# Moving one block of the softmax sums from TensorE to GpSimd, and the FFN bias adds from GpSimd to VectorE

## The chip, the cores and the metric

The kernel runs on one core of a Trainium2 chip. Its time is the device time of one launch in microseconds (us). TensorE is called PE here, VectorE DVE, ScalarE ACT, GpSimd POOL, and SyncE, which issues most DMAs, SP. A difference is told as a share of the time before.

## The reference

A "macaron" layer over 16 sequences of 512 tokens and width 128: half an FFN, causal attention with 16 heads and a latent of 32, half an FFN. Each part has its own layer norm and a residual.

```python
def ffn(x):   # weights rounded to int4, plus a low-rank term
    return einsum('bsd,df->bsf', x, int4(kernel)) + bias + einsum('bsr,rf->bsf', einsum('bsd,dr->bsr', x, a), b)

def attn(x):
    q = einsum('bld,dhk->blhk', x, Wq); lat = einsum('bld,dc->blc', x, Wkv_down)
    k, v = einsum('blc,chk->blhk', lat, Wk_up), einsum('blc,chk->blhk', lat, Wv_up)
    p = softmax(where(causal, einsum('bqhd,bkhd->bhqk', q, k) / 8, -inf))
    return einsum('bqhd,hdo->bqo', einsum('bhqk,bkhd->bqhd', p, v), Wout)

x = x + 0.5 * ffn(layernorm(x))
x = x + attn(layernorm(x))
x = x + 0.5 * ffn(layernorm(x))
```

## The kernel before

**Work and steps.** All is float32. A sequence has four blocks of 128 queries (or keys), and its 16 heads form four groups of four heads. Two groups make a pair, so there are 32 pairs. A pair takes five steps (`STEP`), and the loop over `n` walks through the 160 steps of all pairs. Step `n` computes scores with the queries on the partitions for pair `at(n)`; DVE finds their row maxima (`find_maxima`, L642 and L646, tile `nmax`). Six steps later (`LAG`) the scores are computed again with the keys on the partitions, the maxima are folded in, and ACT takes the exponentials (`exponentials`, L655, tiles `pt`). POOL sets the upper triangle of diagonal blocks to zero (`zeros`, L668, an affine select). PE's part of a step is one `burst` (L632); behind it stand other products: values (tile `o`), sums (tile `s`), projections (`yp`), queries (`qt_ps`), FFN products (`fp_a`, `fp_c`).

**The sums.** A softmax needs the sum of the probabilities over the keys. POOL first adds the tiles of different key blocks, and PE then sums over the partitions with a matrix of ones (`sum_products`, L754, tile `s`). The causal mask leaves query block i with i+1 key blocks. For one group, PE streams: block 0 of `pt0` (128 columns for each of four heads), the three blocks of `b01` (384 columns), which holds key blocks 0 and 1 and, in its middle block, also key block 2; and `b23` (128 columns), which holds key blocks 2 and 3 for the last queries. The products of `b01` and `b23` add up in the same PSUM columns for these queries. POOL makes `b01` with `add_01` (L738, two adds of 128x768) and `add_2` (L743), and `b23` with `add_23` (L748). A pair has `u` = 0 (its first group) and `u` = 1.

**After the sums.** ACT copies them (`ssb`), SP moves them through DRAM in several DMAs, DVE takes reciprocals (L822), SP spreads them over the partitions (`rb`), and POOL multiplies (`normalise`, L830, tile `ot`).

**The FFNs.** `front(b)` (first FFN, letter a) and `tail(b)` (second FFN, letter c) are generators whose pieces are hung into the steps by `plan` and by lists such as `FRONT_STEPS` and `TAIL_STEPS`. `with_bias` (L379, tile `xb`, 128x512) adds the bias to the residual. In `front` it stands in a step of its own, 28 steps ahead of the sequence's first. In `tail` it stands in the same step as `turn_blocks` (L366), the transpose that makes `xt_c`, and ahead of it; the product `fp_c` (L385) reads `xt_c` and stands behind the next burst, and DVE then makes `x3` from `fp_c` and `xb` (L397). Each engine works through its instructions in the order in which the program issues them. `ln_newton` (L344 to L346, tiles `e_w`, `r_w`) is a chain of three small DVE instructions, once per sequence.

**Buffers that matter here.** The score tiles `sx` have two buffers of two PSUM banks; all other PSUM tiles share four banks in turn (`ps_t`). `b01`, `b23` and `xb` have two buffers each.

Of the kernel before, what the change touches and what calls it, by code (L numbers as in the profile page):

```python
# [14 lines left out]
ALU = mybir.AluOpType  # L15
# [10 lines left out]
def macaron_kernel(  # L26
# [14 lines left out]
    nc = tc.nc  # L41
# [43 lines left out]
    def load_x(b):  # L85
        x_sb = io.tile([P, NT, D], F32, tag="x", name=f"x_{b}")
        nc.sync.dma_start(x_sb, x[b].rearrange("(t p) d -> p t d", p=P))
        return x_sb
# [234 lines left out]
    def ln_stats(src, ln, what, blocks):  # L323
        c = COLUMNS[what]
        for t in blocks:
            nc.vector.bn_stats(ln["stats"][:, c + t, :], src[:, t, :])
        for t in blocks:
            nc.vector.bn_aggr(ln["mv"][:, c + t, :], ln["stats"][:, c + t, :])
# [48 lines left out]
    def with_bias(src, name, engine):  # L377
        xb = act2.tile([P, NT, D], F32, tag="xb", name=f"xb_{name}")
        engine.tensor_tensor(xb, src, bias_bc, ALU.add)  # L379
        return xb  # L380
# [25 lines left out]
    def ln_of(what, b):  # L406
        w = b + {"c": 2, "b": -2, "a": -3}[what]
        if w not in lns:
            lns[w] = ln_tile(f"w{w}")
        return lns[w]  # L410
# [10 lines left out]
    def front(b, st):  # L421


        x_sb, z = xs.pop(b), zs.pop(b)
        na, nb = f"a{b}", f"b{b}"
        la = ln_of("a", b) if b > 2 else early["a", b]
        lb = ln_of("b", b) if b > 1 else early["b", b]
        ln_stats(x_sb, la, "a", (0, 1))
        yield
        ln_stats(x_sb, la, "a", (2, 3))  # L430
        if b > 1:
            yield
        if 0 < b < B - 1:
            xs[b + 1] = load_x(b + 1)
            zs[b + 1] = load_blocks(x[b + 1], f"a{b + 1}")
        yield
        if b == 0:
            xt = turn(x_sb, na, "xt_a")
            yield
        xb = with_bias(x_sb, na, nc.gpsimd if b > 1 else nc.vector)  # L440
        yield
        if b:
            xt = turn_blocks(z, na, "xt_a")
            yield
        x1 = st["x1"] = ffn(xt, la, xb, na, "x1", 5)
        yield
        ln_stats(x1, lb, "b", (0, 1))
        yield
        ln_stats(x1, lb, "b", (2, 3))
        yield  # L450
        xn = ln_scale(x1, nb, lb)
        if b:
            there = to_dram(xn, nb)
            yield
            z = load_blocks(there, nb)
        yield
        xnt = turn_blocks(z, nb, "xnt_b") if b else turn(xn, nb, "xnt_b")
        yield
        mp = take(f"kt_ps_{b}")
        kt = st["kt"] = act2.tile([P, L], F32, tag="kt", name=f"kt_{b}", bufs=3)  # L460
        if b == 0:
            product(mp, wkv4_flat, xnt)
            nc.vector.tensor_copy(kt, mp)
        else:

            for j in range(NT):
                nc.tensor.matmul(
                    mp[ts(j, LD), :P], lhsT=wkv4_flat[:, :LD], rhs=xnt[:, ts(j, P)], start=True, stop=True,
                    skip_group_check=True,
                )  # L470
            kt4 = act2.tile([P, P], F32, tag="kt4", name=f"kt4_{b}", bufs=1)
            nc.vector.tensor_copy(kt4, mp[:, :P])
            yield
            kt_d = dram.tile([P, P], F32, tag="kt_d", name=f"kt_d_{b}", bufs=2)
            nc.sync.dma_start(kt_d, kt4)
            yield
            for h in range(HG):
                nc.sync.dma_start(
                    kt[ts(h, LD), :].rearrange("c (j n) -> c j n", j=NT), kt_d.rearrange("(j c) n -> c j n", j=NT)
                )  # L480

        def query(g):
            mp = take(f"qt_ps_{b}_{g}")
            product(mp, wqk_flat[:, ts(g, P)], xnt)
            if g % 2 == 0:
                st["qt", g] = act2.tile([P, 2, L], F32, tag="qt", name=f"qt_{b}_{g}", bufs=4)
            nc.scalar.copy(st["qt", g - g % 2][:, g % 2, :], mp)  # L487

        yield
        query(0)  # L490
        yield
        query(1)
        yield
        query(2)
        yield
        query(3)
        yield
# [18 lines left out]
    def tail(b, st, late=False):  # L516


        x2 = io.tile([P, NT, D], F32, tag="x2", name=f"x2_{b}")
        nm = f"c{b}"  # L520
        ln = ln_tile(nm) if late else ln_of("c", b)
        for half in (0, 1):
            yp = take(f"yp_{b}_{half}")[:, : 2 * D]
            for t in (0, 1):
                for g in range(NG):
                    product(yp[:, ts(t, D)], st["ot"][:, g, ts(2 * half + t, P)], wvo[:, g, :],
                            t == 0 and g == 0, g == NG - 1)
            nc.vector.tensor_tensor(
                x2[:, ts(half, 2), :], yp.rearrange("p (t d) -> p t d", d=D), st["x1"][:, ts(half, 2), :], ALU.add
            )  # L530
            if half and not late:
                there = to_dram(x2, nm)
            yield
            ln_stats(x2, ln, "c", (2 * half, 2 * half + 1))
            yield
        if late:
            xt = turn(x2, nm, "xt_c")
            yield
            ln_rstd(ln, "c")
            yield  # L540
            ln_newton(ln, "c")
        else:
            z = load_blocks(there, nm)
            yield
        xb = with_bias(x2, nm, nc.gpsimd)
        yield
        if not late:
            xt = turn_blocks(z, nm, "xt_c")
            yield
        x3 = ffn(xt, ln, xb, nm, "x3", 3)  # L550
        if not late:
            yield
        nc.sync.dma_start(out[b].rearrange("(t p) d -> p t d", p=P), x3)
        yield
# [190 lines left out]
    def add_23(st, g, u):  # L745

        both = st["b23", g + u] = probs.tile([P, HG, P], F32, tag="b23", name=f"b23_{st['b']}_{g + u}")
        nc.gpsimd.tensor_tensor(both, st["pt", 2, g][:, 2 + u], st["pt", 1, g + u][:, 0], ALU.add)  # L748

    def blocks(dst, w, tile_, start=False):  # L750

        for h in range(HG):
            mv = tile_[:, :, h, :]
            nc.tensor.matmul(  # L754
                dst[ts(h, LD), :].rearrange("p (b n) -> p b n", n=P), lhsT=w[h] if isinstance(w, list) else w,
                rhs=mv, start=start, stop=True, skip_group_check=True,
            )
# [14 lines left out]
            st["osb", g + u] = act2.tile([P, L], F32, tag="osb", name=f"osb_{st['b']}_{g + u}", bufs=4)  # L772
            nc.scalar.copy(st["osb", g + u], o_ps)  # L773

    def sum_products(st, g, u, s_ps):
        g1, w = g + u, ones_f[:, :LD]
        blocks(s_ps[:, :P], w, st["pt", 0, g1][:, :1], start=True)
        blocks(s_ps[:, P:], w, st["b01", g1])
        blocks(s_ps[:, 384:], w, st["b23", g1].unsqueeze(1))

    def sums(st, g, u):

        b, g1 = st["b"], g + u
        s_ps = take(f"s_{b}_{g1}")
        sum_products(st, g, u, s_ps)
        ssb = act2.tile([P, L], F32, tag="ssb", name=f"ssb_{b}_{g1}", bufs=3)
        nc.scalar.copy(ssb, s_ps)
        sums_d = dram.tile([HG, L], F32, tag="sums", name=f"sums_{b}_{g1}")
        for h in range(HG):
            nc.sync.dma_start(sums_d[h : h + 1], ssb[h * LD : h * LD + 1, :])  # L790
        st["sums", g1] = small.tile([P, HG * L // P], F32, tag="sum", name=f"sum_{b}_{g1}")
        nc.sync.dma_start(st["sums", g1], sums_d.rearrange("h n -> (h n)").rearrange("(p n) -> p n", p=P))
# [73 lines left out]
    N = len(groups)  # L866
    STEPS = len(STEP)
# [83 lines left out]
    def due(n, k, lag=LAG):  # L951

        at_ = at(n, lag + k)
        return at_ if at_ and (n - lag - k) % STEPS == 0 else None
# [5 lines left out]
    def ready_work(n):  # L960

        if n < N * STEPS and due(n, 10):
            st, g = due(n, 10)
            normalise(st, g + 1)
        for u in range(2):
            if due(n, 2 + 3 * u):
                st, g = due(n, 2 + 3 * u)
                add_01(st, g + u, 0)
                add_01(st, g + u, 1)
            if due(n, 3 + 2 * u):  # L970
                add_2(*due(n, 3 + 2 * u), u)
            if due(n, 3 + u):
                add_23(*due(n, 3 + u), u)

    for n in range(N * STEPS):
        parts(n - 0.5)
# [16 lines left out]
        for u in range(2):  # L993
            if due(n, 6 + 2 * u):
                st, g = due(n, 6 + 2 * u)
# [6 lines left out]
    n = N * STEPS  # L1002
# [24 lines left out]
    next(late_tail)  # L1027
    o_ps, s_ps = bank("o_late"), bank("s_late")
    values(st, g, 0, o_ps)
    sum_products(st, g, 0, s_ps)  # L1030
    normalise(st, gp)
    divided(turned(st)[:, g, :], o_ps, s_ps)

# [70 lines left out]
```

## Time and profile before

| what | value |
|---|---|
| time, median of 3 runs | 813.44 us (812.99 to 813.50) |
| the profiled execution: its time, its span | 811.2 us, 809.5 us |
| mean granted TensorE clock | 0.984 |
| ACT busy | 488.1 us (60%) |
| PE, products of `s` from `b01` and `b23` (L754) | 65.1 us busy, 992 records |
| POOL `add_01`, 128x768 (L738) | 126 instructions, mean 1820 ns |
| POOL `normalise` (L830) | 62 instructions, mean 1275 ns, 30.4 us idle before them for the DMA of `rb` |

The times and rows of the profile come from the profiled execution. A group's row gives the busy time, then the mean duration of one instruction, then the idle time of the engine before these instructions and what ended it. A float32 matmul leaves two records. A matmul's records overlap with the next ones', so starts tell more than durations there. In a timeline the first column is the start and the second the duration of a run of equal instructions.

### The profile page before, as it was taken

Reading aid. Unit: us, or ns where it says so; the run is one execution under the profiler, and the core shown is the slowest. Engines: PE = TensorE matmul, PEld = TensorE weight load, DVE = VectorE, ACT = ScalarE, POOL = GpSimd, SP = SyncE. Lnnn points to the kernel's source line nnn. Section 1 sums busy time; section 2 is a strip of 40 time slices with the busy share of each in tenths; the row PEclk is TensorE's granted clock in tenths of the full one; section 3 lists DMA queues with packets and bytes.
Section 4 is the critical chain, followed back from the end, with each engine's and each line's share of the span. In section 5 each row is a group of like instructions: output and inputs, shape, how many; then the busy total and the mean of one; then the engine's idle time right before and its main releaser. Section 6 shows DMA issues by size and latency. Waiting matters only on the chain.

```text
span 809.5 us, 35716 instructions
## 1 busy us (share of the span) xinstructions
PE 785.4 (97%) x15400; PEld 508.6 (63%) x15400; DVE 618.8 (76%) x1317; ACT 488.1 (60%) x971; POOL 677.6 (84%) x676
## 2 busy tenths in 40 slices
PE   7899999999999999999999999999999999999986
PEld 5646566676666667666666666566666766666544
DVE  7787886878778697777879787777878777686716
ACT  1247675757566675756667575666657566575652
POOL 1018989999998999989999998989989989989991
PEclk7899999999999999999999999999999999999998
DMA  6123122233322324232332323223122222211211
GB/s 138 28 60 65 35 69 68 62 72 77 91 64 67 85 58 93 64 82 60 82 84 56 88 60 83 73 70 83 51 67 68 50 72 70 60 45 56 45 38 34
DMA packets 171022, 54.01 MB, mean 67 GB/s; under 512 B 119512, under 2 KB 162680, under 8 KB 170864
## 3 DMA queue, kind: packets, MB, share of 16 engines
q1 hardware_dynamic: 170096, 51.44, 26.9%
q8 instruction: 120, 1.97, 1.0%
q10 hardware_dynamic: 768, 0.30, 0.2%
q14 instruction: 38, 0.31, 0.1%
HBM read 37.90 MB, written 13.80 MB: 64 GB/s over the span
## 4 chain that ended last, share of the span: by engine, by line
PE 77%; DVE 7%; DMA 4%; ACT 4%; POOL 4%; issue 2%; SPq 1%; DVEq 0%; POOLq 0%; ACTq 0%
PE sx L632 18%; PE o L754 15%; PE tx L632 14%; PE s L754 8%; PE yp L385 6%; PE qt_ps L385 6%; DVE nmax L642 2%; POOL b L738 2%; PE fp_a L385 2%; PE fp_c L385 2%; ACT xn_b L355 2%; DMA rb<-recs 2%; DMA recs<-rec 2%; ACT pt L655 1%; POOL ot L830 1%
## 5 line engine op out<-in xcount | busy, mean ns | idle before, releaser
L642 DVE TENSOR_REDUCE nmax<-sx 128x2 f32<-128x768 f32 (+2 forms) x384 | 312.6, 863 | 104.9 <-PE tx L632 66.8
L655 ACT ACTIVATE pt<-tx 128x512 f32<-128x512 f32 x616 | 319.5, 598 | 86.0 <-PE tx L632 78.8
L632 PE MATMUL sx<-kt,qt 32*128 32x512 f32 (+3 forms) x2048 | 323.4, 442 | 0.0
L632 PE MATMUL tx<-qt,kt 32*128 32x512 f32 x1728 | 319.2, 469 | 0.0
L738 POOL TENSOR_TENSOR b<-pt,pt 128x768 f32<-128x768 f32 x126 | 226.7, 1820 | 0.5
L632 PEld LDWEIGHTS sx<-kt,qt 32*128 32x128 f32 x2048 | 176.0, 185 | 24.4 <-issue 0.4
L668 POOL TENSOR_SCALAR_AFFINE_SELECT pt<-pt 128x1024 f32<-128x1024 f32 (+1 forms) x162 | 144.8, 899 | 19.8 <-ACT pt L655 17.6
L754 PE MATMUL o<-pt,lat 128*32 128x512 f32 x1984 | 146.4, 435 | 0.8 <-POOL pt L668 0.8
L632 PEld LDWEIGHTS tx<-qt,kt 32*128 32x128 f32 x1728 | 131.5, 185 | 5.1
L754 PEld LDWEIGHTS o<-pt,lat 128*32 128x32 f32 x1984 | 62.5, 109 | 77.9 <-issue 59.0
L632 PE MATMUL tx<-rows,ones_u 6*128 6x512 bf16 (+1 forms) x988 | 109.7, 297 | 1.0 <-DVE wvo L292 0.5
L830 POOL TENSOR_TENSOR ot<-osb,rb 128x512 f32<-128x512 f32 x62 | 79.1, 1275 | 30.5 <-DMA rb<-recs 30.4
L646 DVE TENSOR_REDUCE nmax<-sx 128x4 f32<-128x1024 f32 x64 | 75.4, 1219 | 31.7 <-PE tx L632 31.4
L773 ACT COPY osb<-o 128x512 f32<-128x512 f32 x62 | 36.3, 585 | 92.1 <-PE o L754 92.1
L632 PE MATMUL sx<-eye_b,mask_w 32*128 32x64 bf16 (+1 forms) x2560 | 87.6, 183 | 2.7 <-DVE nmax L646 1.7
L632 PEld LDWEIGHTS <-ones_u 6*128 6x128 bf16 x1024 | 43.1, 92 | 74.3 <-issue 61.6
L632 PEld LDWEIGHTS <-mask_w 32*128 32x128 bf16 x2560 | 67.3, 92 | 32.9 <-issue 24.7
L743 POOL TENSOR_TENSOR b<-b,pt 128x512 f32<-128x512 f32 x63 | 80.5, 1278 | 5.1
L748 POOL TENSOR_TENSOR b<-pt,pt 128x512 f32<-128x512 f32 x63 | 80.4, 1277 | 0.1
L385 PE MATMUL qt_ps<-xnt_b_b,wqk 128*32 128x512 f32 x512 | 68.0, 603 | 0.2
L754 PE MATMUL s<-b,ones_f 128*32 128x384 f32 x992 | 65.1, 380 | 2.2 <-POOL b L743 2.1
L487 ACT COPY qt<-qt_ps 128x512 f32<-128x512 f32 x64 | 37.5, 586 | 47.3 <-PE qt_ps L385 47.2
(193 smaller groups left out, 818.0 us busy)
## 6 DMA issues: line engine op xcount, KB each, us to landing
rb<-recs SPq DMA_DIRECT2D x248, 64.0 KB
x<-in_x_dram SPq DMA_DIRECT2D x16, 256.0 KB
sums<-ssb SPq DMA_DIRECT2D x248, 2.0 KB
z_a<-in_x_dram SPq DMA_DIRECT2D x60, 64.0 KB
blocks_b<-xn_b SPq DMA_DIRECT2D x15, 256.0 KB
z_b<-blocks_b SPq DMA_DIRECT2D x60, 64.0 KB
kt<-kt_d SPq DMA_DIRECT2D x60, 64.0 KB
out_dram<-x_c SPq DMA_DIRECT2D x15, 256.0 KB
```

Of the source, the lines that this page charges most:

```text
L385: nc.tensor.matmul(dst[ts(h, LD), :], lhsT=w[:, ts(h, LD)], rhs=mv, start=start, stop=stop, skip_group_check=True)
L487: nc.scalar.copy(st["qt", g - g % 2][:, g % 2, :], mp)
L632: nc.tensor.matmul(dst, lhsT=w, rhs=mv, start=first, stop=last, skip_group_check=True)
L642: nc.vector.tensor_reduce(nmax[:, i, heads, u], sx[:, :, col : col + (i + 1) * P], AX.X, ALU.max, negate=True)
L646: nc.vector.tensor_reduce(nmax[:, 1, heads, :], sx.rearrange("p k (u n) -> p k u n", u=2), AX.X, ALU.max, negate=True)
L655: nc.scalar.activation(pt[:, :, 2 * pair + k, :], tx[k].rearrange("p (b n) -> p b n", n=P), AF.Exp)
L668: nc.gpsimd.affine_select(diag, diag, pattern=[[0, diag.shape[1]], [1, P]], compare_op=ALU.is_ge, fill=0.0, base=0, channel_multiplier=-1,)
L738: nc.gpsimd.tensor_tensor(*flat, ALU.add)
L743: nc.gpsimd.tensor_tensor(b01, b01, st["pt", 2, g][:, u], ALU.add)
L748: nc.gpsimd.tensor_tensor(both, st["pt", 2, g][:, 2 + u], st["pt", 1, g + u][:, 0], ALU.add)
L754: nc.tensor.matmul(dst[ts(h, LD), :].rearrange("p (b n) -> p b n", n=P), lhsT=w[h] if isinstance(w, list) else w, rhs=mv, start=start, sto ...
L830: nc.gpsimd.tensor_tensor(turned(st)[:, g, :], st["osb", g], st["rb", g], ALU.mult)
```

## The change

For the first group of a pair (`u` = 0), and only inside the loop over `n`, POOL adds `b23` onto the last block of `b01` in place (`add_0123`), issued behind the `add_23` of that step; the sums of that group then leave out the product of `b23`. Sums of second groups, and of the very last pair (`late`), are as before. The bias adds of both FFNs move from POOL to DVE: all of `front`, and those of `tail` but the one of sequence 14 (`late`). The first two of `front` were on DVE already.

```diff
-        xb = with_bias(x_sb, na, nc.gpsimd if b > 1 else nc.vector)
+        xb = with_bias(x_sb, na, nc.vector)
...
-        xb = with_bias(x2, nm, nc.gpsimd)
+        xb = with_bias(x2, nm, nc.gpsimd if late else nc.vector)
...
+    def add_0123(st, g):
+
+        b01 = st["b01", g][:, 2]
+        nc.gpsimd.tensor_tensor(b01, b01, st["b23", g], ALU.add)
...
-    def sum_products(st, g, u, s_ps):
+    def sum_products(st, g, u, s_ps, late=False):
         g1, w = g + u, ones_f[:, :LD]
         blocks(s_ps[:, :P], w, st["pt", 0, g1][:, :1], start=True)
         blocks(s_ps[:, P:], w, st["b01", g1])
-        blocks(s_ps[:, 384:], w, st["b23", g1].unsqueeze(1))
-
-    def sums(st, g, u):
+        if u == 1 or late:
+            blocks(s_ps[:, 384:], w, st["b23", g1].unsqueeze(1))
+
+    def sums(st, g, u, late=False):
...
                 add_23(*due(n, 3 + u), u)
+        if due(n, 3) and n < N * STEPS:
+            add_0123(*due(n, 3))
...
-    sum_products(st, g, 0, s_ps)
+    sum_products(st, g, 0, s_ps, True)
```

More of the change, by code (lines that the diff above doesn't have):

```diff
@@ L778, in sum_products @@
         blocks(s_ps[:, P:], w, st["b01", g1])
-        blocks(s_ps[:, 384:], w, st["b23", g1].unsqueeze(1))
-    def sums(st, g, u):
+        if u == 1 or late:
+            blocks(s_ps[:, 384:], w, st["b23", g1].unsqueeze(1))
+    def sums(st, g, u, late=False):
         b, g1 = st["b"], g + u
         s_ps = take(f"s_{b}_{g1}")
-        sum_products(st, g, u, s_ps)
+        sum_products(st, g, u, s_ps, late)
         ssb = act2.tile([P, L], F32, tag="ssb", name=f"ssb_{b}_{g1}", bufs=3)
```

## The prediction, made before the changed kernel ran

> **What bounds the kernel now.** I read the page's busy times first, then PE's groups by form, the timeline around one sums stage, PE's own waits, and last the timelines of DVE and POOL at the places where the bias adds are to stand.
>
> ```profile
> PE 785.4 (97%) x15400; PEld 508.6 (63%) x15400; DVE 618.8 (76%) x1317; ACT 488.1 (60%) x971; POOL 677.6 (84%) x676
> ```
>
> PE is busy for 97% of the span. That alone could be overlap of records, so I looked at starts: over all 62 stages of `o`, for instance, the time from the stage's start to the next stage's start is 2.18 to 2.64 us with a median of 2.29, that is, PE issues without holes. Its listed waits are small:
>
> ```profile
> PE s L754 <- POOL b L743: 2.1, 5, 1.0
> PE sx L632 <- DVE nmax L646: 1.7, 1, 1.7
> ```
>
> (total us, times, longest.) So a stage taken from PE shortens the program unless something new comes late. POOL's `b` is the only input that PE waited for several times, so POOL is the engine to watch.
>
> **What the change removes from PE.** A sums stage of a first group:
>
> ```profile
> 420.89 0.43 PE L754 MATMUL s<-pt,ones_f 128*32 128x128 f32 x8
> 421.14 1.05 PE L754 MATMUL s<-b,ones_f 128*32 128x384 f32 x16
> 422.00 0.41 PE L385 MATMUL mt<-ident_b,terms 128*32 128x128 bf16 x16
> ```
>
> From start to start the products of `b01` and `b23` take 422.00 - 421.14 = 0.86 us for 384 + 128 columns, so the 128 that go take a quarter, 0.215 us; the 128 of `pt` take 0.25 by the same reading. Other ends: 24.9 us busy for the 62 products of this form is 0.40 each, but that includes the drain under which the next stage already runs. I take 0.215. There are 31 such stages (32 pairs less the last): 31 x 0.215 = 6.7 us (7.8 by 0.25).
>
> **What POOL gains and loses.** Rows: `add_0123` has the form of L743.
>
> ```profile
> L743 POOL TENSOR_TENSOR b<-b,pt 128x512 f32<-128x512 f32 x63 | 80.5, 1278 | 5.1
> L379 POOL TENSOR_TENSOR xb_a<-x,bias_sb 128x512 f32<-128x512 f32 x14 | 17.8, 1268 | 17.8 <-DVE x_a L397 17.8
> L379 DVE TENSOR_TENSOR xb_a<-x,bias_sb 128x512 f32<-128x512 f32 x2 | 1.4, 684 | 0.0
> ```
>
> Added 31 x 1.278 = 39.6 us, removed 28 bias adds (14 of each FFN) x 1.268 = 35.5; net 4.1 of 677.6. In the order of instructions a bias add goes from in front of `add_01` of the first group, and the new add comes behind `add_23` of the same group, so within most pairs POOL runs 1.27 us ahead in between and is back in place after it. Where no bias add goes (the first pairs, some of the last), POOL is 1.3 us late from the new add on. Who waits for that: the sums of `u` = 0, one burst later. Between the end of `add_23` and PE's start on `b01` there are 1.81 us in the tightest of the 31 pairs (68.59 to 70.41) and up to 5.7, so 1.3 fits. Behind the new add queue the small casts of `terms`, the next select, `ot` and the second group's adds. There the cover is a wait that POOL has anyway:
>
> ```profile
> 447.46 1.28 POOL L830 TENSOR_TENSOR ot<-osb,rb 128x512 f32<-128x512 f32 x1 [1.50 <-DMA rb<-recs]
> ```
>
> This wait is 0.3 to 2.3 us in most pairs; PE then has 0.05 to 1.8 us until it needs the second group's `b01`. Without cover a pair would lose up to 1.3.
>
> **What DVE gains.** 28 x 0.684 = 19.2 us at 76% busy. But does an add of two SBUF tensors run at that pace beside POOL? The two above ran while POOL was idle. The trace has such instructions beside POOL's adds, the `e_w` chain:
>
> ```profile
> 424.48 3.62 POOL L738 TENSOR_TENSOR b<-pt,pt 128x768 f32<-128x768 f32 x2
> 426.27 1.85 DVE L344 SCALAR_TENSOR_TENSOR e_w<-mv_w,y_w 128x12 f32<-128x12 f32 x1
> 428.17 1.29 POOL L743 TENSOR_TENSOR b<-b,pt 128x512 f32<-128x512 f32 x1
> 428.37 1.13 DVE L346 SCALAR_TENSOR_TENSOR r_w<-e_w,y_w 128x12 f32<-128x12 f32 x1
> ...
> 796.25 0.16 DVE L344 SCALAR_TENSOR_TENSOR e_c<-mv_c,y_c 128x4 f32<-128x4 f32 x1 [4.10 <-ACT y_c L339]
> ```
>
> L344 takes 0.16 us with POOL idle and 1.85 here: it ends at 428.12, as POOL's second add ends at 428.10. L346 ends with L743. So a DVE instruction with two SBUF inputs that finds a POOL add running waits for its end, up to 1.82 us, and gets in ahead of the next. Whether POOL's add in turn waits for a long DVE instruction, these 0.16 us ones cannot show: between nothing and 0.68 us per bias add. I take the whole; POOL is then 0.69 us late per pair instead of level, which the wait for `rb` covers in all but about the last two pairs.
>
> [...]
>
> **The first FFN's add** is issued behind the transpose of `xnt_b`, at about 408.3 in the pair at 400. POOL's add of 128x768 will then run from 407.7 to 409.5, so the bias add ends near 410.1, and the four maxima of the step, 409.65 to 412.13 before, end at 413.3. PE's next burst starts at 413.26 on the buffer whose maxima come first (by 412.3). Cover 1 us; without it the burst waits. No cost.
>
> **The second FFN's add** is the tight one, for the transpose of `xt_c` is right behind it, and `fp_c` waits for that.
>
> ```profile
> 429.42 2.34 DVE L646 TENSOR_REDUCE nmax<-sx 128x4 f32<-128x1024 f32 x2
> 430.88 1.09 POOL L668 TENSOR_SCALAR_AFFINE_SELECT pt<-pt 128x1024 f32<-128x1024 f32 x1 [0.83 <-ACT pt L655]
> 431.68 0.70 DVE L366 STREAM_TRANSPOSE xt_c_c<-z_c 128x512 f32<-128x512 f32 x1
> 431.94 1.27 POOL L379 TENSOR_TENSOR xb_c<-x,bias_sb 128x512 f32<-128x512 f32 x1
> 434.13 1.08 PE L385 MATMUL fp_c<-w_mid,xt_c_c 128*32 128x128 f32 x32
> ```
>
> DVE comes to it at 431.68, while POOL's select runs until 431.97; POOL's next add of 128x768 now starts right there. In the 14 places DVE is there 0.2 to 0.9 us before the select's end. Whether the select holds it or not, it is ahead of the add: bias add until 432.65 at the latest, transpose until 433.3, 0.8 us before `fp_c`. The maxima start at 433.45 instead of 433.09, which nothing feels. Three of the 14 have only 0.2 us, and bursts now come 0.2 earlier; for those and for the uncovered last pairs I charge 0.6.
>
> **Sum.** 811.2 - 6.7 + 0.6 = 805.1 for an execution like the profiled one. That one is 2.2 us below the median of the runs; against 813.44 the forecast is 807.3.
>
> **Rivals.**
> 1. *The second FFN's add comes behind POOL's add (slower).* If DVE arrives after the select's end, it waits 1.82, ends at 434.4, the transpose at 435.0: `fp_c` is 0.9 late. Behind it the maxima and `x3` end at 438.7 instead of 436.6, and the burst's second half, due at 437.07 + 0.9, takes over `fp_c`'s bank: 0.7 more. 1.6 x 14 = 22 us, so 829 if it hits every sequence, 818 if half. It decides at a shift of 0.2 to 0.9 us between DVE and POOL. For it: the `e_w` chain just ahead, itself held by POOL, sets DVE's arrival. Against: the shift is on the good side in all 14. 0.25.
> 2. *The second groups' sums come late:* the cover by the wait for `rb` fails since that DMA chain does not get faster with PE. PE's gain of 0.215 per pair then goes into the wait of L754 for L743, plus up to 0.7 in pairs without slack: 813 to 818. Against: the wait is POOL's, not PE's, in 29 of 62. 0.08.
> 3. *The gain is real and elsewhere eaten to nothing,* DVE at 79% holding `sx` a little longer in each sequence: 0.24 each in 28 places is 6.7, so 813.4. 0.05.
>
> **Chances.** Forecast 0.62. A measurement here tells about 0.2%, 1.6 us, from no change. Faster: 0.62 and a little of rival 1 where few places are hit, 0.64. Within 0.2%: rival 3 and some of 2, 0.07. Slower: 0.29. Range: from 805.0 (7.8 us gained, nothing lost, rounded down) to 820, which takes in rivals 2 and 3 and half of rival 1; about 0.15 is left out above.
>
> **What would show it.** Right: 248 records fewer of the 128x128 product `s<-b`; first groups' stages 0.64 us from `b01` to the next stage; POOL's L379 nearly gone; DVE's `xb_a` near 1.8 us, `xb_c` near 1; the step from `fp_c`'s stage before to `fp_c` unchanged. Wrong: `xb_c` above 2 us and PE waiting for DVE before `fp_c` (rival 1), or PE's wait of L754 for L743 well above 2.1 us (rival 2).

## The result, and the profile after

The changed kernel has a median of 811.41 us in 20 runs (809.42 to 813.75), the kernel before 813.38 in 20 (810.78 to 814.91): ratio 0.9981, interval 0.9972 to 0.9990. It is faster by about 1.6 to 2.0 us. The sum forecast 6.1. The direction came out, two thirds of the gain did not.

The page's row of engines (busy us, share, instructions):

```profile
PE 782.2 (96%) x15152; PEld 503.0 (62%) x15152; DVE 646.9 (80%) x1345; ACT 486.3 (60%) x971; POOL 691.1 (85%) x679
```

PE has 248 records fewer, as forecast, DVE 28 us more. A first group's stage in the timeline of PE:

```profile
422.42 0.43 PE L759 MATMUL s<-pt,ones_f 128*32 128x128 f32 x8
422.66 0.83 PE L759 MATMUL s<-b,ones_f 128*32 128x384 f32 x8
423.31 0.41 PE L385 MATMUL mt<-ident_b,terms 128*32 128x128 bf16 x16
```

From `b01` to the next stage it is 423.31 - 422.66 = 0.65 us, 0.86 before. Compared stage by stage with the trace of before, PE comes 0.215 us earlier at every one of these places but the first, that of pair 0, where the next stage waits. So the gain was there and was given back elsewhere. PE's waits (total us, times, longest):

```profile
PE s L759 <- POOL b L743: 4.4, 8, 1.0
...
PE mt L385 <- POOL terms L723: 1.7, 3, 1.0
...
PE o L759 <- POOL pt L668: 1.5, 3, 1.0
```

Before, these were 2.1, 1.2 and 0.8. The first is the wait that the prediction put up as the sign of its rival 2. The list takes in only part of it, since PE's weight loads wait too (for the same `b` 4.3 us before and 7.3 after). Taken instead as the step from the product of `pt` to that of `b01` in the second groups' sums, less 0.24 (undisturbed it is 0.22 to 0.24), the delay sums to 3.5 us before and 6.2 after. Below this is the second groups' delay. In both traces 1.2 us of it are those of the last such sums, at 777 us. POOL's own waits:

```profile
POOL terms L719 <- DVE nmax L642: 47.6, 1, 47.6
POOL ot L836 <- DMA rb<-recs: 21.2, 22, 1.7
```

The wait for `rb` is still there (30.4 before). In the pairs where POOL waits for it, POOL is not late by its own work. All delayed pairs but the last, ten of them, are of this kind: POOL stood idle for 0.9 to 1.7 us before the `ot` that precedes their adds.

The spans of the two profiled executions, 811.1 us and 809.5, would say that the changed kernel is slower. They differ at the head. These are windows of the trace; after the span come the busy times of PE, PEld, DVE, ACT and POOL, then the granted clock, DMA share and GB/s; first before, then after:

```profile
26.00:34.00 8.00, 7.07 (x105) 3.54 (x104) 4.95 (x12) 2.18 (x5) 0.00 (x0) 1.00 0.21 35
```

```profile
26.00:34.00 8.00, 7.33 (x84) 3.01 (x83) 3.37 (x10) 1.67 (x4) 0.00 (x0) 0.79 0.21 35
```

The granted clock was 1.00 in one and 0.79 in the other, and PE is 2.6 us later at 42 us. Of the experiments below, e11 (bias adds on POOL) had 0.79 there too, e10 (bias adds on DVE) 1.00. So it is no effect of the change, and PE's progress is compared from behind the head on.

### The profile page after: what moved, and what is told of

Read it like the earlier page. It is cut to its first block, busy times and chain, and to the rows that moved or that the text cites. A ratio compares the mean times of both kernels' runs of the same rounds, so it can differ in the third digit from the quotient of the medians.

```text
span 811.1 us, 35275 instructions
## 1 busy us (share of the span) xinstructions
PE 782.2 (96%) x15152; PEld 503.0 (62%) x15152; DVE 646.9 (80%) x1345; ACT 486.3 (60%) x971; POOL 691.1 (85%) x679
## 4 chain that ended last, share of the span: by engine, by line
PE 61%; POOL 16%; DVE 9%; DMA 5%; ACT 3%; issue 3%; SPq 2%; POOLq 0%; DVEq 0%; ACTq 0%
PE sx L632 14%; PE o L759 12%; PE tx L632 11%; POOL b L738 7%; PE yp L385 6%; PE s L759 5%; PE qt_ps L385 5%; DVE nmax L642 3%; DMA rb<-recs 3%; POOL pt L668 2%; POOL b L743 2%; POOL ot L836 2%; PE fp_a L385 2%; SPq L833 1%; ACT xn_b L355 1%
## 5 line engine op out<-in xcount | busy, mean ns | idle before, releaser
L642 DVE TENSOR_REDUCE nmax<-sx 128x2 f32<-128x768 f32 (+2 forms) x384 | 310.3, 858 | 78.9 <-PE tx L632 45.9
L738 POOL TENSOR_TENSOR b<-pt,pt 128x768 f32<-128x768 f32 x126 | 235.0, 1885 | 2.7
L759 PE MATMUL s<-b,ones_f 128*32 128x384 f32 x744 | 58.4, 416 | 4.5 <-POOL b L743 4.4
```

Source lines behind the costliest of these rows:

```text
L642: nc.vector.tensor_reduce(nmax[:, i, heads, u], sx[:, :, col : col + (i + 1) * P], AX.X, ALU.max, negate=True)
L738: nc.gpsimd.tensor_tensor(*flat, ALU.add)
L759: nc.tensor.matmul(dst[ts(h, LD), :].rearrange("p (b n) -> p b n", n=P), lhsT=w[h] if isinstance(w, list) else w, rhs=mv, start=start, sto ...
```

## The experiments

Ratios are to runs of the kernel before taken beside those of the experiment, with 95% intervals. "Drift" is by how much a stage of PE starts later than in the trace of before.

**Which part gives the gain back?** e1 is the new add alone:

```diff
-        xb = with_bias(x_sb, na, nc.vector)
+        xb = with_bias(x_sb, na, nc.gpsimd if b > 1 else nc.vector)
...
-        xb = with_bias(x2, nm, nc.gpsimd if late else nc.vector)
+        xb = with_bias(x2, nm, nc.gpsimd)
```

> The new add and the shorter first-group sums alone; both bias adds stay on POOL as in the kernel before. POOL gets 31 x 1.28 = 40 us more and nothing back. Theory (POOL's chain makes the second groups' sums late): the whole 1.28 us now stands in front of the second group's adds, so PE's waits for them grow by more than in the changed kernel (there from 3.5 to 6.2 us): 812 to 818, ratio 0.998 to 1.006. Rival A (the loss is at DVE's places: the head's xb_a in front of xt_a, about 1 us, and the bursts): these are as before here, so the gain is larger than the changed kernel's: 807 to 809, ratio 0.992 to 0.995.

Measured 1.0025 (1.0013 to 1.0036), 816.25 us. POOL is now busy for 715.2 us. PE's waits:

```profile
PE o L759 <- POOL pt L668: 4.2, 9, 1.2
PE s L759 <- POOL b L743: 3.6, 9, 0.8
PE mt L385 <- POOL terms L723: 2.8, 3, 2.1
```

The add without the bias moves costs more than the 6.7 us that it takes from PE. POOL is late with everything that it makes, `pt` and `terms` too. So the bias moves are needed to pay for it. The time came out as expected, but not by the expected wait: the second groups' delay is 5.3 us in this trace, less than the changed kernel's 6.2, and what grew is the waits for `pt` and `terms`.

e2 is the bias moves alone: `add_0123` is not issued, and the sums of both groups stream `b23`.

```diff
-        if u == 1 or late:
+        if True:
             blocks(s_ps[:, 384:], w, st["b23", g1].unsqueeze(1))
...
-        if due(n, 3) and n < N * STEPS:
-            add_0123(*due(n, 3))
```

> The bias adds on DVE alone; all sums stream five blocks as before and there is no new add. PE's work is that of the kernel before. Theory (POOL's chain): POOL is ahead by up to 1.27 us less the hold of 0.3 per bias add, so the second groups' waits of 3.5 us mostly go, and the head loses about 1: 811 to 813, ratio 0.997 to 0.9995. Rival A (DVE's adds cost the time): 815 to 817, ratio 1.002 to 1.005. Rival B (bias adds cost and free nothing that PE feels): ratio 1.000.

Measured 1.0008 (0.9995 to 1.0021): no difference. The theory as I had it missed here. POOL was 23 us less busy than before (654.6 against 677.6), yet the second groups' delay did not go; it is 5.1 us in this trace, against 3.5. A POOL with more room does not make these sums earlier.

e3 is the changed kernel without the add:

```diff
-        if due(n, 3) and n < N * STEPS:
-            add_0123(*due(n, 3))
```

> The changed kernel without POOL's new add: the first groups' sums leave the product of b23 out and nothing puts it back, so that part of the sum is missing. PE has the changed kernel's work, POOL 40 us less. Theory (the new add makes the second groups' sums late): nearly the whole 6.7 us show, less about 1 us at the head: 807 to 808, ratio 0.992 to 0.994. Rival A (DVE's places cost it): as slow as the changed kernel, 810.5 to 811.5, ratio 0.996 to 0.998.

Measured 0.9956 (0.9942 to 0.9971), 3.6 us below before, between the two expectations. The second groups' delay is 5.6 us, nearly that of the changed kernel, though POOL is busy for 37 us less (654.5 against 691.1). So most of it is not the new add's. The trace shows whose it is. Pair 18 (from 0), delayed by 0.6 us before and by 1.0 in the changed kernel; its main lines before:

```profile
488.09 0.22 DVE L822 RECIPROCAL rec<-sum 128x16 f32<-128x16 f32 x1
495.00 1.28 POOL L830 TENSOR_TENSOR ot<-osb,rb 128x512 f32<-128x512 f32 x1 [2.26 <-DMA rb<-recs]
499.92 1.27 POOL L743 TENSOR_TENSOR b<-b,pt 128x512 f32<-128x512 f32 x1
501.24 1.07 PE L754 MATMUL s<-b,ones_f 128*32 128x384 f32 x16 [0.39 <-POOL b L743]
```

and in the changed kernel's timelines:

```profile
489.58 0.22 DVE L828 RECIPROCAL rec<-sum 128x16 f32<-128x16 f32 x1
489.82 0.34 SPq L830 DMA_DIRECT2D recs<-rec  x1
492.92 1.69 SPq L833 DMA_DIRECT2D rb<-recs  x4
496.40 1.28 POOL L836 TENSOR_TENSOR ot<-osb,rb 128x512 f32<-128x512 f32 x1 [1.74 <-DMA rb<-recs]
497.64 3.59 POOL L738 TENSOR_TENSOR b<-pt,pt 128x768 f32<-128x768 f32 x2
501.31 1.27 POOL L743 TENSOR_TENSOR b<-b,pt 128x512 f32<-128x512 f32 x1
501.39 0.40 PE L759 MATMUL s<-pt,ones_f 128*32 128x128 f32 x8
502.63 1.07 PE L759 MATMUL s<-b,ones_f 128*32 128x384 f32 x16 [0.84 <-POOL b L743]
```

`rec` goes through DRAM and comes back as `rb`; POOL's `ot` waits for it, and behind `ot`, in POOL's order, stand the second group's two `add_01` and `add_2`. `add_2` ends 6.2 us after `ot` starts (6.17 to 6.22) in every pair but the last. From `rec` to `ot` it is 5.1 to 7.3 us, in no fixed order, in 120 pairs of five traces (before, after, e1 to e3; pairs 4 to 27, counted from 1). In 16 of these, 11 of them e1's, POOL came later than the transfer; where it waited, the range is 5.1 to 7.2. The sums of the second group start 12.36 or 12.42 us after `rec` in most pairs of the kernel before, and want the last add 0.22 after their own start. A transfer of over 12.36 - 6.19 + 0.22 = 6.39 us therefore delays PE. PE's shorter first group lies between `rec` and these sums, so in the changed kernel 12.36 becomes about 12.1 and the threshold 6.15. Over the 120 times, 32% exceed 6.39 and 40% exceed 6.15; the mean excess times 31 pairs is 3.1 and 5.7 us. The traces have 3.5 and 6.2; without the 1.2 of the last sums, which this does not explain, 2.3 and 5.0. One trace alone scatters: e2, whose sums stand where they stood before, has 5.1. So 2.6 us, from the 120 times, is the firmer figure for what the moved threshold costs; the difference of two traces agrees with it, but can be off by 1 or 2 us.

e4 takes the wait away from the front of these adds, by issuing `ot` behind them:

```diff
 def ready_work(n):
-        if n < N * STEPS and due(n, 10):
-            st, g = due(n, 10)
-            normalise(st, g + 1)
...
             if due(n, 3 + u):
                 add_23(*due(n, 3 + u), u)
         if due(n, 3) and n < N * STEPS:
             add_0123(*due(n, 3))
+        if n < N * STEPS and due(n, 10):
+            st, g = due(n, 10)
+            normalise(st, g + 1)
```

> The changed kernel with POOL's product of the older pair's second group (ot, which waits for the rb transfer) issued behind the second group's adds instead of in front of them. Theory: POOL comes to add_01 of the second group 1.3 us and the rb wait earlier, so the 6.2 us of waits for those sums fall under 1 us: 806 to 808.5, ratio 0.991 to 0.994. Rival A (the loss is not in that wait): ratio 0.997 to 0.999. Rival C (ot later makes something else late: the two projections that read ot, or the osb and rb buffers): slower than the changed kernel.

Measured 0.9986 (0.9974 to 0.9998): no better than the changed kernel. The second groups' delay did fall, to the 1.2 us of the last sums, but `ot` is now too late for the projections that read it. The stage of `yp` before and in e4:

```profile
451.99 1.95 PE L385 MATMUL yp<-wvo,ot 128*32 128x128 f32 x64
453.76 0.40 PE L754 MATMUL s<-pt,ones_f 128*32 128x128 f32 x8
```

```profile
453.70 2.27 PE L385 MATMUL yp<-wvo,ot 128*32 128x128 f32 x64
455.79 0.40 PE L759 MATMUL s<-pt,ones_f 128*32 128x128 f32 x8
```

It takes 455.79 - 453.70 = 2.09 us, against 1.77 before, and this comes back once per sequence. The wait has only changed its place, as the last rival of that text had it.

**`ot` between.** e10 puts it between `add_01` and `add_2`:

```diff
-        if n < N * STEPS and due(n, 10):
-            st, g = due(n, 10)
-            normalise(st, g + 1)
...
+            if u and n < N * STEPS and due(n, 10):
+                st, g = due(n, 10)
+                normalise(st, g + 1)
             if due(n, 3 + 2 * u):
                 add_2(*due(n, 3 + 2 * u), u)
```

> The changed kernel with POOL's ot of the older pair's second group between the second group's add_01 and add_2: behind the rb transfer's usual landing, ahead of the projections that read it. Theory (a pair's second-group sums end a fixed 6.2 us after rb lands, rb lands 5.1 to 7.2 us after rec, and PE's shorter pair only moves the deadline closer): the sums' waits of 6.2 us go and so do the 0.31 us that the projections waited for ot in e4: 5 to 6 us better than the changed kernel, ratio to the kernel before 0.990 to 0.993. Rival (POOL as a whole is now the bound, whatever its order): no better than the changed kernel, 0.997 to 0.999.

Measured 0.9929 (0.9912 to 0.9946), 807.46 us, as the theory said. The same pair in e10's timelines:

```profile
484.96 0.22 DVE L828 RECIPROCAL rec<-sum 128x16 f32<-128x16 f32 x1
490.00 3.62 POOL L738 TENSOR_TENSOR b<-pt,pt 128x768 f32<-128x768 f32 x2
493.56 1.28 POOL L836 TENSOR_TENSOR ot<-osb,rb 128x512 f32<-128x512 f32 x1
494.78 1.30 POOL L743 TENSOR_TENSOR b<-b,pt 128x512 f32<-128x512 f32 x1
497.06 0.40 PE L759 MATMUL s<-pt,ones_f 128*32 128x128 f32 x8
497.28 1.05 PE L759 MATMUL s<-b,ones_f 128*32 128x384 f32 x16
```

`ot` comes 8.6 us after `rec`, later than any transfer took, and waits for nothing; `add_2` ends 1.2 us before PE's `b01`. From the second pair to the 26th, PE's drift now falls by 0.215 in every pair, and by more where the kernel before had waited. The 4.2 us from the changed kernel's ratio to this one fit the 5.0 us of delay that went, within the intervals.

e11 is the kernel before with that one move:

> The kernel before with that one move of ot and nothing else. Theory: its waits for second-group sums (3.5 us in the profile; 3.1 by the spread of the transfers' times) go, but for the 1.2 of the last pair: ratio 0.996 to 0.998. Rival (the waits are not the transfer's): 0.9995 to 1.0005.

Measured 0.9968 (0.9957 to 0.9980): 2.6 us. So the kernel before lost time in the same place. Against e11, the change as a whole (e10) is worth 0.9929 / 0.9968 = 0.996 (0.994 to 0.998 from the two intervals).

e12 is e10 without the new add:

> e10 without POOL's new add: the first groups' sums lack the product of b23, so that part of the sum is missing. If the move takes all dependence on POOL away, this is as fast as e10 within 0.1% (0.990 to 0.992); if POOL's load still matters there, it is over 0.2% faster than e10.

Measured 0.9909 (0.9890 to 0.9929); 7.4 us below before. From the second pair to the last, its drift falls by 8.26 us and e11's by 2.04: the difference, 6.2 us, is 29 times 0.215. PE's gain is real and whole where nothing takes it. The intervals of e10 and e12 overlap, so the two times do not settle what the add costs; the drifts do: from the first pair's values to the last second group's sums, 6.41 us in e10 and 8.00 in e12, so 1.6 us. All of it arises in pairs 0, 26, 28 and 30 (pairs counted from 0 from here on).

e14 is e10 with both bias adds on POOL, as in e1:

> e10 with both bias adds back on POOL. Theory (POOL has the room once it doesn't wait for rb): POOL's 40 us more take the place of the 30 us that it waited, so the sums are late again in part: 0.994 to 0.999. Rival (bias adds on DVE are what costs, 1 us at the head and more): as fast as e10 or faster, 0.988 to 0.991.

Measured 0.9965 (0.9952 to 0.9978), worse than e10: POOL has no room for 40 us more without the bias moves even when it does not wait for `rb`. The sums are not late again, against my theory: the second groups' delay is 0.0 us. PE waits for POOL's `terms` (3.2 us in its list) and for the select's `pt` (2.4) instead.

**The rest.** e13 is e10 with one bias add, that of block 2's first FFN, on POOL:

```diff
-        xb = with_bias(x_sb, na, nc.vector)
+        xb = with_bias(x_sb, na, nc.gpsimd if b == 2 else nc.vector)
```

> e10 with the bias add of block 2's first FFN back on POOL (the one that stands in front of the transpose of xt_a at 42 us). Theory (that add holds PE's fp_a at the head back by 0.5 to 1.0 us, and the loss stays to the end): 0.5 to 1.0 us better than e10, ratio to the kernel before 0.9915 to 0.9925; in the trace fp_a at 42 us no later than before. Rival (the stage behind it takes the delay up, or POOL's later row costs as much): as e10, 0.993.

Measured 0.9911 (0.9893 to 0.9928); it cannot be told from e10, and from the second pair on its drift is the same, -7.0 us in both. I had taken a loss of 1 us at `fp_a` (42 us) for that add's. The traces of e1, e11 and e14, which have it on POOL, show the same 0.98 to 0.99 there: it goes with the low clock at the head (0.79 from 26 to 34 us in e11). In e10, whose clock there was that of before, 0.5 us appear at 42 us and are gone again at 46.

e15 is e10 without the add in pairs 0, 26, 28 and 30, whose first groups stream `b23`:

```diff
-        if due(n, 3) and n < N * STEPS:
+        if due(n, 3) and n < N * STEPS and groups.index(due(n, 3)) not in (0, 26, 28, 30):
             add_0123(*due(n, 3))
...
-                sums(*due(n, 4 + 2 * u), u)
+                sums(*due(n, 4 + 2 * u), u, groups.index(due(n, 4 + 2 * u)) in (0, 26, 28, 30))
...
-    sums(st, gp, 0)
+    sums(st, gp, 0, True)
```

> e10 with the new add left out in pairs 0, 26, 28 and 30, whose first groups stream b23 as before. These are the pairs in which no first FFN's bias add leaves POOL; in e10's trace PE loses 0.2 to 0.6 us in each behind them, in e12's (no add at all) it doesn't. Theory (there POOL only gains work, and its chain is late): 4 x 0.22 lost on PE, about 1.6 won: 0.8 us better than e10, ratio 0.9915 to 0.9925. Rival (the loss there has another cause): 0.9 us worse than e10, 0.994.

Measured 0.9896 (0.9879 to 0.9913), 804.65 us, the fastest version here. Its interval touches e10's; in the drift it gains 0.93 us over e10. PE's waits in e10 and then in e15:

```profile
PE mt L385 <- POOL terms L723: 1.7, 3, 1.0
...
PE o L759 <- POOL pt L668: 1.5, 3, 1.0
```

```profile
PE mt L385 <- POOL terms L723: 0.8, 2, 0.5
...
PE o L759 <- POOL pt L668: 0.4, 1, 0.4
```

Together they fall from 3.2 us to 1.2, below the 2.0 of before. The new add stands ahead of the casts of `terms` and of the select that `values` (tile `o`) needs. That these pairs have no first FFN's bias add to give away, as the text on e15 says, is not the reason: in pairs 26, 28 and 30 a bias add does leave POOL, the second FFN's; pairs 2, 25, 27 and 29 give none away and lose nothing; and e16 below, with the first FFN's adds back on POOL, loses in the same four pairs. The trace of before shows what sets them apart: PE came for these results within less than the add's 1.28 us. In it, the select and `o` of pair 24 and then of pair 26:

```profile
633.03 0.64 POOL L668 TENSOR_SCALAR_AFFINE_SELECT pt<-pt 128x512 f32<-128x512 f32 x1
634.26 1.08 PE L385 MATMUL fp_a<-w_mid,xt_a_a 128*32 128x128 f32 x32
635.15 2.34 PE L754 MATMUL o<-pt,lat 128*32 128x512 f32 x32
```

```profile
680.35 0.63 POOL L668 TENSOR_SCALAR_AFFINE_SELECT pt<-pt 128x512 f32<-128x512 f32 x1
681.26 2.36 PE L754 MATMUL o<-pt,lat 128*32 128x512 f32 x32
```

From the select's end to `o` there are 1.48 us in pair 24, 0.28 in pair 26: the first FFN's product `fp_a`, which stands ahead of `o` up to pair 24, is over. Pair 28 has 0.41 there. Pair 0 has 1.18 us from the end of `terms` to `mt` (1.7 to 2.2 in the other even pairs), and in pair 30 PE already waits for both.

e16 and e17 are e10 with the first or the second FFN's adds back on POOL:

```diff
e16
-        xb = with_bias(x_sb, na, nc.vector)
+        xb = with_bias(x_sb, na, nc.gpsimd if b > 1 else nc.vector)
e17
-        xb = with_bias(x2, nm, nc.gpsimd if late else nc.vector)
+        xb = with_bias(x2, nm, nc.gpsimd)
```

> e10 with the first FFN's 14 bias adds on POOL again, the second's on DVE. Theory (a pair's POOL chain is full once the new add has nothing that goes for it): the pairs with a first FFN's add lose 0.2 to 0.4 of their 0.215, the head wins 0.5 to 1: 0.993 to 0.996. Rival (DVE's xb_a costs more than it frees): 0.990 to 0.992.

> e10 with the second FFN's 14 bias adds on POOL again, the first's on DVE. Theory: as e16, in the other pairs, without the head's gain: 0.994 to 0.997. Rival (DVE's xb_c in front of the transpose of xt_c costs PE time): 0.990 to 0.992.

e16 measured 0.9914 (0.9900 to 0.9928), e17 0.9956 (0.9943 to 0.9969). The second FFN's adds must leave POOL for this change to pay; the first FFN's need not, against my theory, which expected a loss for both. With `ot` between, the pairs with a first FFN's add have slack on POOL: from the fourth pair to the 26th `add_2` ends at least 0.88 us before PE's `b01` in e16, but only 0.55 in every second pair of e17. In e17's trace 0.11 to 0.13 us per sequence goes to an `o` stage, and the waits at the tail grow:

```profile
PE mt L385 <- POOL terms L723: 3.4, 3, 2.6
...
PE o L759 <- POOL pt L668: 2.0, 2, 1.1
```

## Why the prediction was wrong in size, by its own steps

**The gain on PE** (31 x 0.215 = 6.7 us) was right: 0.65 us per stage, 248 records, and the whole of it in e12 against e11.

**"The cover is a wait that POOL has anyway"** is the step that failed. It counted the wait for `rb` as room in which POOL's 0.69 us could vanish, and charged nothing for the sums behind it; its 0.6 us stands for three tight places of the second FFN's add and for the last pairs. POOL's lateness did vanish in that wait. But the wait ends with a transfer whose start PE's order sets and whose length does not shrink (from `rec` to the second groups' `ot`, where POOL waited for it, 5.1 to 7.0 us before and 5.1 to 7.2 in the changed kernel): behind it, what counts is not how late POOL comes but how much of the deadline is left, and the deadline moves up by 0.215 us in every pair. Rival 2 had said exactly this. It got a chance of 0.08, since the waits were POOL's and not PE's, and a size for all pairs. The right size was in the trace of before: from `rec` to `ot` 5.1 to 7.0 us there, over 6.39 in six of the 29 pairs before the last sums, over 6.15 in nine. The term measured 2.7 us (3.5 to 6.2; 2.6 by the 120 times), not nothing and not 6.7. e4 and e10 show that this order of POOL is the cause: two ways to take `rb` from the front of the adds, both of which end the delay but for the last sums, and the one that puts it nowhere else brings the time. Why one transfer takes 2 us longer than another was not tested.

**"Where no bias add goes ... so 1.3 fits"** failed as well. It looked only at the sums of `u` = 0. The add is also ahead of `terms` and of the next select, which `mt` and `o` wait for; that these queue behind it was named, and no room was worked out for them. It also sought the places by where a bias add goes, and they are those where PE comes early. Pairs 0, 26, 28 and 30 cost 1.6 us, shown by e12 and partly won back by e15.

**The first FFN's add, "No cost":** nearly right. One stage at the head (`qt_ps` at 84 us) is 0.39 to 0.48 us late in every trace with the later `xb_a` on DVE and in none with them on POOL. The sign "`xb_a` near 1.8" did not come in the changed kernel, where the 16 take 1.09 us on the mean and two of them over 2: the adds that were held mostly found the select running.

**The second FFN's add** went as worked out, and rival 1, with the chance of 0.25, did not come. Timelines of the pair that the prediction looked at:

```profile
432.19 1.09 POOL L668 TENSOR_SCALAR_AFFINE_SELECT pt<-pt 128x1024 f32<-128x1024 f32 x1 [0.41 <-ACT pt L655]
432.35 1.48 DVE L379 TENSOR_TENSOR xb_c<-x,bias_sb 128x512 f32<-128x512 f32 x1
433.37 3.92 POOL L738 TENSOR_TENSOR b<-pt,pt 128x768 f32<-128x768 f32 x2
433.75 0.70 DVE L366 STREAM_TRANSPOSE xt_c_c<-z_c 128x512 f32<-128x512 f32 x1
435.44 1.08 PE L385 MATMUL fp_c<-w_mid,xt_c_c 128*32 128x128 f32 x32
```

DVE comes while the select runs, is done 0.55 us after it, and the transpose ends 1.0 us before `fp_c`. The adds moved take 0.97 to 1.48 us, near the sign of 1 and below that of rival 1.

**The hold of POOL by DVE** was priced at the whole 0.68 us per add. POOL's two adds here take 3.92 us instead of 3.62, so 0.30. Before and after:

```profile
L738 POOL TENSOR_TENSOR b<-pt,pt 128x768 f32<-128x768 f32 x126 | 226.7, 1820 | 0.5
L738 POOL TENSOR_TENSOR b<-pt,pt 128x768 f32<-128x768 f32 x126 | 235.0, 1885 | 2.7
```

That is 8.3 us more, 0.30 for each of the 28 adds; 25 of POOL's adds are longer, most by 0.31 and two by 0.46. So POOL's adds did lose time to DVE's, but less than the whole: here DVE has 0.46 us left when POOL's first add starts (433.37 to 433.83), and the two adds are longer by 0.30, two thirds of that; why was not tried.

Together: -6.7 + 2.7 + 1.6 + 0.4 = -2.0 us, against a measured 0.8 to 2.3 less (0.9972 to 0.9990). The changed kernel's own trace has 1.0 less from 42 us to the end; the difference is in places of about 0.2 us each (`kt_ps` at 237 us, `fp_c` at 803) that I did not follow up. Rival 3 did not happen: PE's waits for the maxima of L642 are 1.3 us after and 1.0 before.

## What to carry to other kernels

Do not count a wait for a transfer on an engine as a cushion for the work behind it; here that left out 2.7 us. List the spread of the transfer's times, work out from which length on the consumer is late, and when the consumer gets faster, move that threshold: the cost is estimated by what the mean excess over it grows by (here 2.6 us, with 2.7 measured), not nothing and not the whole gain (6.7). An instruction that waits for a transfer belongs behind work that does not need it, but ahead of whoever reads its result; here that one move alone (0.9968) brought at least as much as the change under study (0.9981).

Where a change adds work to an engine, go through all that is queued behind it there, not only the reader of its result, and through the rounds in which those readers come earlier than in the steady ones (first and last).

## What the runs showed of the hardware that I had not expected

A DVE add of two SBUF tensors was held by a running one-input select on POOL too: the 1.48 us above, 0.65 to 0.68 undisturbed. In return it lengthened POOL's adds by only 0.3 us in most places, less than half of its own time.

The way from `rec` through DRAM and back varies by up to 2 us (5.1 to 7.2, where POOL waited for it) from pair to pair within one execution, with the same instructions each time.

The granted clock between 26 and 34 us is 1.00 in some executions (before, e10, e13) and 0.79 in others (the changed kernel, e11, e16, e17) of nearly the same program, and PE is 1.9 to 2.6 us later at 42 us in the traces with 0.79, and at most 1.0 later in those with 1.00, than in the trace of before. Why it differs was not tested. Two profiled spans of this kernel can therefore not be compared directly at the level of 0.3% (2.6 us of 811).
